# Two cross-attention layers on one core: two products split a second time, bias sums moved to ScalarE and DMA, first loads reordered

## The chip, the core and the metric

The kernel runs on one core of a Trainium2 chip. The metric is the time on the device in microseconds (us): 641.56 as the median of three runs (641.52 to 641.75). All data are float32.

TensorE (PE; its weight loads are shown as PEld) multiplies into PSUM, VectorE (DVE) and ScalarE (ACT) work on SBUF and PSUM, GpSimd (POOL) on SBUF. SyncE (SP), ScalarE and GpSimd issue DMAs. Each engine takes its instructions from a queue of its own.

## The reference

Eight batches of 100 queries with 1024 features attend to 1444 context rows with 512 features, twice. The second layer has no output product, and it normalises its result.

```
# layer 0
Q = x @ Wq + bq;  K = ctx @ Wk + bk;  V = ctx @ Wv + bv
w = softmax(Q @ K.T / 32, axis=-1)          # over the context
x = x + (w @ V) @ Wo + bo
# layer 1
q = x @ Wq + bq;  k = ctx @ Wk + bk;  v = ctx @ Wv + bv
w = softmax(q @ k.T / 32, axis=1)           # over the queries
y = w @ v + x
out = (y - mean(y)) * rsqrt(var(y) + 1e-6) * gamma + beta
```

## The kernel before

The scores need only Wq Wk^T (1024 x 512) and not Wq and Wk each, so the kernel multiplies weights first: **qk0** = Wq Wk^T of layer 0, **vo0** = Wv Wo (512 x 1024), and later **qk1** = Wq Wk^T of layer 1. The biases enter as vectors: Wq bk, Wk bq and Wo^T bv. The stages are qk0, vo0, the projected queries g0 of layer 0 (`queries`), qk1, the rounds of layer 0 (in each, `alternated` interleaves the weighted sum A of one batch, L531, with the scores s of the batch two further on, L560), the output product of layer 0, the projected queries of layer 1, the rounds of layer 1, and the normalisation.

**Seven products instead of eight.** Each weight product (`weight_products`, L241) is cut in quarters A11 .. A22 and B11 .. B22 and computed by Strassen's method in Winograd's form. The products are called X, Z, Y, W, and X again twice and Y again, as two banks of PSUM are used once more; the results that are finished in between are copied out by ScalarE (`put`, L296) or added by VectorE (`add`, L301). The sums and differences of quarters (`combine`, L165) are VectorE's. For qk0 and qk1 a product is sixteen matmuls of 256 columns, for vo0 eight of 512. The order on TensorE is the program's:

```
X = A11 B11;  Z = A12 B21;  Y = S1 T1;  W = A22 T4;  X += S2 T2;  X += S3 B12';  Y += S4 B22
```

with S1 = A21 + A22, T1 = B12 - B11, T2 = B22 - T1, T4 = B21 - T2, S2 = S1 - A11, S3 = A11 - A21, S4 = A12 - S2. Most sums overwrite a quarter that is not needed any more. An "X +=" goes into banks that `put` has just copied, so its first matmul waits for that copy. The last "X +=" (line L348) is called V below.

**Loads.** The contraction of 1024 is cut in eight units (tag `unit`, ten buffers), each with its rows of the left and the right matrix; a unit of a later product is loaded when a buffer is free. All these loads are issued by SyncE, except the first two by ScalarE (L254). For qk0 they come in the order of L255 to L263: left half and the whole right row of each unit, then the second left halves.

**Bias vectors.** `accumulate` (L305) multiplies each unit by a column of the bias and adds up the eight units on VectorE, one instruction for each (L318, L320), in rows of 1024 (tag `row`, three buffers) or 512. `block_sums` (L355) transposes blocks of 32 and reduces them, and `totals` (L363) sums over the partitions with a matmul on TensorE.

TensorE's order is the program's (`manual_schedule`). On the other engines a scheduler places instructions by priority and expected readiness, except those passed through `keep_in_program_order`. A buffer of a tag is free when its last reader is done. The tiles `prob` (three) hold scores; their rows from 96 on and their columns from 1444 on are cleared by GpSimd at the start (L135, L136). `weight_rows` (tag `wT`, three buffers) are used from the first softmax on.

Of the kernel before, what the change touches and what calls it, by code (L numbers as in the profile page):

```python
# [25 lines left out]
F32 = mybir.dt.float32  # L26
AF = mybir.ActivationFunctionType
# [28 lines left out]
def two_layer_cross_attention(ctx: ExitStack, tc: tile.TileContext, a: dict, out: bass.AP):  # L56
# [11 lines left out]
    def bank(name):  # L68
        return psum.tile([P, 512], F32, tag="ps", name=name)

    def bank2(name):
        return psum2.tile([P, 512], F32, tag="ps2", name=name)
# [59 lines left out]

    prob = [const.tile([P, SW], F32, tag=f"prob{n}", name=f"prob{n}") for n in range(3)]
    for t in prob:
        nc.gpsimd.memset(t[T // QD * QD :, :], 0.0)  # L135
        nc.gpsimd.memset(t[:, S:], 0.0)  # L136

    def run(*parts):

        parts = list(parts)  # L140
        while parts:
            parts = [g for g in parts if next(g, parts) is not parts]
# [7 lines left out]

    def half_product(banks, lhs, rhs, fresh, nb, width):

        per = nb // len(banks)
        for i in range(len(lhs)):
            for n in range(nb):
                nc.tensor.matmul(  # L156
                    banks[n // per][:, n % per * width : (n % per + 1) * width],
                    lhs[i][:, n * P : (n + 1) * P],
                    rhs[i],
                    start=(fresh and i == 0 and n % per == 0),  # L160
                    stop=(i == len(lhs) - 1),
                    skip_group_check=True,
                )

    def combine(to, x, y, op, engine=vector):  # L165
        for t, p, q in zip(to, x, y):
            engine.tensor_tensor(t, p, q, op)
# [19 lines left out]
    def seven_products(name, A, Bs, S, T_, nb, width, put, add, left=None, right=None):  # L187
# [49 lines left out]
        add(0, 1, Y)  # L237
        yield


    def weight_products(name, left, right, l_width, r_width, scaled):  # L241

        H, lh, rh = EC // 2, l_width // 2, r_width // 2
        nb, per = lh // P, 512 // rh
        lsrc = a[left].rearrange("(p c) n -> p c n", c=EC)
        rsrc = a[right].rearrange("(p c) n -> p c n", c=EC)  # L250
        units = [unit(f"{name}_{h}") for h in range(EC)]
        if name == "qk0":
            for part in (slice(0, lh // 2), slice(lh // 2, lh)):
                nc.scalar.dma_start(out=units[0][:, part], in_=lsrc[:, 0, part])  # L254
            nc.sync.dma_start(out=units[0][:, l_width : l_width + rh], in_=rsrc[:, 0, :rh])  # L255
            for h in range(1, EC):
                nc.sync.dma_start(out=units[h][:, :lh], in_=lsrc[:, h, :lh])
                nc.sync.dma_start(out=units[h][:, l_width : l_width + r_width], in_=rsrc[:, h, :])
                if h == 1:
                    nc.sync.dma_start(out=units[0][:, l_width + rh : l_width + r_width], in_=rsrc[:, 0, rh:])  # L260
            for i in range(H):
                for h in (i, H + i):
                    nc.sync.dma_start(out=units[h][:, lh:l_width], in_=lsrc[:, h, lh:])  # L263
        else:
            for h in range(EC):
                nc.sync.dma_start(out=units[h][:, :l_width], in_=lsrc[:, h, :])
                nc.sync.dma_start(out=units[h][:, l_width : l_width + r_width], in_=rsrc[:, h, :])

        def lefts(k, j):
            return [units[k * H + i][:, j * lh : (j + 1) * lh] for i in range(H)]  # L270

        def rights(k, j):
            return [units[k * H + i][:, l_width + j * rh : l_width + (j + 1) * rh] for i in range(H)]

        A11, A12, A21, A22 = lefts(0, 0), lefts(1, 0), lefts(0, 1), lefts(1, 1)
        B11, B12, B21, B22 = rights(0, 0), rights(0, 1), rights(1, 0), rights(1, 1)
        extra = [wide(f"{name}_s{n}").rearrange("p c t -> p (c t)") for n in range(2)]
        S1 = [extra[i // 2][:, i % 2 * 768 : i % 2 * 768 + lh] for i in range(H)]
        T1 = [extra[i // 2][:, i % 2 * 768 + lh : (i % 2 + 1) * 768] for i in range(H)]

        dst = weights.tile([P, l_width // P, r_width], F32, tag="w", name=name)

        def pair(n):
            return [(bank2 if n == "w" else bank)(f"{name}_{n}{j}") for j in range(2)]

        def product(banks, lhs, rhs, fresh):
            half_product(banks, lhs, rhs, fresh, nb, rh)

        def block(r, c, j):

            n = r * nb + j * per
            return dst[:, n : n + per, c * rh : (c + 1) * rh]

        def put(r, c, banks):
            for j in range(2):
                nc.scalar.copy(block(r, c, j), banks[j].rearrange("p (n w) -> p n w", n=per))  # L296

        def add(r, c, banks):
            for j in range(2):
                to = block(r, c, j)  # L300
                nc.vector.tensor_tensor(to, to, banks[j].rearrange("p (n w) -> p n w", n=per), ALU.add)  # L301

        accs = {}

        def accumulate(side):  # L305
            for v, of in scaled:
                if of != side:
                    continue
                width = (l_width, r_width)[side]
                if width == E:  # L310
                    acc = row(f"{name}_{v}")
                else:
                    acc = work.tile([P, L], F32, tag="half", name=f"{name}_{v}", bufs=1)
                accs[v] = acc
                for h in range(EC):
                    src = units[h][:, :l_width] if side == 0 else units[h][:, l_width : l_width + r_width]
                    if h == 0:
                        nc.vector.tensor_scalar(acc, src, cols[v][:, h : h + 1], None, ALU.mult)  # L318
                    else:
                        nc.vector.scalar_tensor_tensor(acc, src, cols[v][:, h : h + 1], acc, ALU.mult, ALU.add)  # L320

        X = pair("x")
        product(X, A11, B11, True)
        put(0, 0, X)
        combine(T1, B12, B11, ALU.subtract)
        combine(S1, A21, A22, ALU.add)
        Z = pair("z")
        product(Z, A12, B21, True)
        accumulate(1)
        add(0, 0, Z)  # L330
        Y = pair("y")
        product(Y, S1, T1, True)
        put(1, 1, Y)
        combine(B11, B22, T1, ALU.subtract)
        T2 = B11
        combine(B21, B21, T2, ALU.subtract)
        W = pair("w")
        product(W, A22, B21, True)
        put(1, 0, W)
        combine(S1, S1, A11, ALU.subtract)  # L340
        S2 = S1
        combine(B12, B22, B12, ALU.subtract)
        product(X, S2, T2, False)
        put(0, 1, X)
        accumulate(0)
        combine(A21, A11, A21, ALU.subtract)
        combine(A12, A12, S2, ALU.subtract)
        product(X, A21, B12, False)  # L348
        add(1, 0, X)
        add(1, 1, X)  # L350
        product(Y, A12, B22, False)
        add(0, 1, Y)
        return dst, [accs[v] for v, _ in scaled]

    def block_sums(name, t, sums):  # L355

        nc.vector.transpose(t, t)  # L360
        nc.vector.tensor_reduce(sums, t.rearrange("p (c q i) -> p c q i", q=P // QD, i=QD), AX.X, ALU.add)

    def totals(name, sums, n):  # L363
# [10 lines left out]
    def quarter_sums(name):  # L374
        return small.tile([P, 2 * EC, P // QD], F32, tag="sums", name=f"{name}_sums")
# [87 lines left out]
    for g in range(B // G):  # L463
# [9 lines left out]
    block_sums("wqbk0", acc_c, sums_c[:, :EC, :])  # L473
    gT = [None, None]
    gT[0], steps = queries(0, wqk0, totals("u0", sums_u, LC))
    run(steps)
    block_sums("bvo", acc_o, sums_c[:, EC:, :])
    got = totals("wqbk0", sums_c, 2 * EC)
    wqbk0 = got[:, :EC]
    nc.vector.tensor_tensor(out_bias, out_bias, got[:, EC:], ALU.add)  # L480
    kb0 = [key_bias_sums(f"kb0_{g}", g * GT, (g + 1) * GT, wqbk0) for g in range(B // G)]
    wqk1, (acc_c, acc_u) = weight_products(
        "qk1", "L1_xattn_WqT", "L1_xattn_WkT", E, L, (("L1_xattn_bk", 0), ("L1_xattn_bq", 1))
    )
    c0 = key_biases("c0", kb0, bqbk0)
    for e in range(EC):
        nc.gpsimd.tensor_scalar(xT[:, e, :], xT[:, e, :], out_bias[:, e : e + 1], None, ALU.add)  # L487
    sums = quarter_sums("k1")
    block_sums("u1", acc_u, sums[:, :LC, :])
    block_sums("wqbk1", acc_c, sums[:, LC : LC + EC, :])  # L490
    got = totals("k1", sums[:, : LC + EC, :], LC + EC)
    u1, wqbk1 = got[:, :LC], got[:, LC:]


    def load_features(b):

# [345 lines left out]
    for b in range(B):  # L842
        if b == B - 1:

            o0 = list(project0(AS, A0))
            next(o0[0])
            next(o0[0])
        run(alternated(b, 0, softmax0, A0[b // G][:, :, b % G * T : (b % G + 1) * T]))
        if b == 1:
            AS = value_sums(wvo)  # L850
    next(o0[1])
    for steps in o0:
# [67 lines left out]
```

## Time and profile before

| what | us |
|---|---|
| median of three runs | 641.56 |
| the profiled execution | 642.15 |
| its span, first to last instruction | 640.30 |
| TensorE busy | 628.8 |
| VectorE busy | 457.0 |
| ScalarE busy | 132.1 |
| GpSimd busy | 101.8 |

The mean granted clock of TensorE was 0.996. Busy time by stage, from the windows of the trace (columns: stretch, its length, PE, DVE, ACT, POOL busy, DMA in GB/s):

| stretch | stage | length | PE | DVE | ACT | POOL | GB/s |
|---|---|---|---|---|---|---|---|
| 0 to 20.9 | qk0, X and Z | 20.9 | 17.86 | 13.58 | 2.46 | 8.82 | 313 |
| 20.9 to 55.8 | qk0, the rest | 34.9 | 34.90 | 33.66 | 3.52 | 0.00 | 240 |
| 55.8 to 104.2 | vo0 | 48.4 | 48.40 | 40.74 | 4.69 | 0.00 | 126 |
| 104.2 to 142.0 | g0 | 37.8 | 37.80 | 25.37 | 4.76 | 0.00 | 72 |
| 142.0 to 190.7 | qk1 | 48.7 | 48.70 | 34.09 | 4.69 | 20.82 | 77 |
| 190.7 to 210.4 | first scores | 19.7 | 19.70 | 8.53 | 6.95 | 0.00 | 354 |
| 210.4 to 232.0 | round 0 | 21.6 | 21.60 | 16.22 | 6.82 | 0.00 | 277 |
| 232.0 to 254.0 | round 1 | 22.0 | 22.00 | 12.13 | 7.79 | 0.00 | 314 |

How to read it: the times of a row are of one execution under the profiler. A matmul of float32 shows as two records. The ends of matmuls are modelled, and the records of neighbours overlap, so the length of a stage is better read from the chain of work than from a sum of records. "Idle before" in a row is the time its engine stood before it, with what released it.

### The profile page before, as it was taken

To read this page: it belongs to the slowest core of one execution; us is meant where nothing else is said; L and a number is where in the kernel's file an instruction comes from. 1 tells how busy PE (TensorE), PEld (TensorE's weight loads), DVE (VectorE), ACT (ScalarE), POOL (GpSimd) and SP (SyncE) were. 2 spreads that over 40 slices of the span, in tenths; PEclk is the share of its full clock that TensorE was granted. 3 is DMA by queue.
4 is the path that set the end of the run, shared out by engine and by line. 5 is a ranking of instruction groups with operands and counts; after the bars stand their busy time and mean duration, and the time that the engine had idled before them with its cause. 6 is when DMAs were issued, how large, how long until landed. Compare 5 with 4: busy or idle time off the path is not lost.

```text
span 640.3 us, 9944 instructions
## 1 busy us (share of the span) xinstructions
PE 628.8 (98%) x3968; PEld 518.0 (81%) x3968; DVE 457.0 (71%) x864; ACT 132.1 (21%) x337; POOL 101.8 (16%) x118
## 2 busy tenths in 40 slices
PE   8999999999999999999999999999999999999994
PEld 7886445568885999999998655556999999999992
DVE  5999959569823775666655798229786659898886
ACT  1010010100103333212330000123332340325301
POOL 5000000009200000000010000007212220454054
PEclk9999999999999999999999999999999999999998
DMA  9928019000079799899896303046788990599002
GB/s 290 384 86 333 0 49 340 0 1 0 2 268 364 264 320 302 306 314 323 300 336 214 126 1 131 2 156 212 265 308 306 310 321 35 193 329 333 28 20 83
DMA packets 47907, 127.28 MB, mean 199 GB/s; under 512 B 3890, under 2 KB 6450, under 8 KB 47862
## 3 DMA queue, kind: packets, MB, share of 16 engines
q1 hardware_dynamic: 45784, 120.85, 54.6%
q0 software_dynamic: 1680, 5.33, 2.4%
q8 instruction: 31, 0.51, 0.3%
q10 hardware_dynamic: 398, 0.47, 0.2%
q14 instruction: 14, 0.11, 0.1%
HBM read 123.36 MB, written 3.28 MB: 198 GB/s over the span
## 4 chain that ended last, share of the span: by engine, by line
PE 94%; DVE 2%; issue 1%; DMA 1%; POOL 1%; POOLq 0%; SPq 0%; ACT 0%; DVEq 0%
PE s L560 25%; PE A L531 24%; PE qk_x L156 5%; PE g_x L156 5%; PE o_x L156 5%; PE qk_y L156 4%; PE g_y L156 3%; PE vo_x L156 3%; PE o_y L156 3%; PE qk_w L156 2%; PE vo_y L156 2%; PE g_w L156 2%; PE g_z L156 2%; PE o_w L156 2%; PE o_z L156 2%; PE qk_z L156 1%
## 5 line engine op out<-in xcount | busy, mean ns | idle before, releaser
L531 PE MATMUL A<-w,c 120*128 120x100 f32 (+1 forms) x1536 | 247.5, 265 | 0.0
L531 PEld LDWEIGHTS A<-w,c 120*128 120x128 f32 (+1 forms) x1536 | 215.9, 190 | 0.8
L93 DVE STREAM_TRANSPOSE w<-prob 32x384 f32<-32x384 f32 (+1 forms) x256 | 143.7, 561 | 37.3 <-ACT prob L572 15.1
L560 PE MATMUL s<-cT,g1T 128*100 128x131 f32 (+2 forms) x592 | 122.8, 297 | 0.0
L560 PE MATMUL s<-cT,g0T 128*100 128x131 f32 (+2 forms) x592 | 122.7, 296 | 0.0
L560 PEld LDWEIGHTS s<-cT,g1T 128*100 128x100 f32 x592 | 78.3, 167 | 8.9 <-ACT g1T L436 0.9
L560 PEld LDWEIGHTS s<-cT,g0T 128*100 128x100 f32 x592 | 78.3, 167 | 8.3
L572 ACT ACTIVATE prob<-s,c 100x393 f32<-100x393 f32 (+2 forms) x64 | 35.1, 560 | 116.7 <-PE s L560 116.4
L682 ACT ACTIVATE w<-w,negmax 120x100 f32<-120x100 f32 (+1 forms) x96 | 34.8, 364 | 82.3 <-DVE negmax L93 82.3
L487 POOL TENSOR_SCALAR xT<-xT,L_xattn_bo 128x800 f32<-128x800 f32 x8 | 20.8, 2609 | 134.0 <-PE qk_x L156 134.0
L592 DVE TENSOR_REDUCE maxima<-prob 100x1 f32<-100x394 f32 (+3 forms) x32 | 16.6, 528 | 28.1 <-ACT prob L572 27.9
L156 PE MATMUL qk_x<-qk 128*128 128x256 f32 x128 | 29.0, 382 | 1.0 <-DMA qk<-in_L_xattn_WkT 1.0
L701 POOL TENSOR_TENSOR part<-w 120x500 f32<-120x500 f32 x8 | 10.9, 1365 | 112.9 <-DVE rstd L776 28.6
L156 PEld LDWEIGHTS qk_x<-qk 128*128 128x128 f32 x128 | 23.7, 190 | 5.3 <-DMA qk<-in_L_xattn_WqT 1.3
L865 POOL DMA_DIRECT2D vectors<-in_L_xattn_gamma x1 | 0.6, 604 | 163.2 <-DMA c<-in_ctx 163.2
L320 DVE SCALAR_TENSOR_TENSOR qk_L_xattn_bk<-qk,L_xattn_bk,qk_L_xattn_bk 128x1024 f32<-128x1024 f32 x14 | 17.9, 1277 | 3.3 <-DMA qk<-in_L_xattn_WqT 3.2
L436 ACT ACTIVATE g1T<-g_x,k 128x400 f32<-128x400 f32 x6 | 3.6, 594 | 74.2 <-PE g_x L156 63.8
L93 DVE TENSOR_TENSOR xT<-xT,o_x 128x400 f32<-128x400 f32 (+1 forms) x32 | 15.9, 540 | 3.9 <-PE o_x L156 3.7
L682 ACT ACTIVATION_READ_ACCUMULATOR w<-w,negmax 120x1 f32 (+1 forms) x96 | 17.9, 187 | 0.0
L781 POOL TENSOR_TENSOR z<-z,vectors 100x1024 f32<-100x1024 f32 x7 | 16.5, 2352 | 8.2 <-ACT z L780 8.2
L759 PE MATMUL z<-ident,xT 128*100 128x128 f32 x64 | 16.3, 273 | 0.0
L93 DVE TENSOR_TENSOR w<-w,rtotal 120x400 f32<-120x400 f32 (+1 forms) x24 | 15.6, 649 | 0.7
(212 smaller groups left out, 869.4 us busy)
## 6 DMA issues: line engine op xcount, KB each, us to landing
cT<-in_ctxT SPq DMA_DIRECT2D x64, 722.0 KB, 6.6
c<-in_ctx SPq DMA_DIRECT2D x48, 768.0 KB, 8.5
c<-in_ctx SPq DMA_DIRECT2D x16, 512.0 KB, 6.8
vo<-in_L_xattn_Wo SPq DMA_DIRECT2D x8, 512.0 KB, 5.4
qk<-in_L_xattn_WqT SPq DMA_DIRECT2D x8, 512.0 KB
qk<-in_L_xattn_WqT SPq DMA_DIRECT2D x15, 256.0 KB, 5.4
qk<-in_L_xattn_WkT SPq DMA_DIRECT2D x15, 256.0 KB, 6.3
c<-in_ctx SPq DMA_DIRECT2D x16, 224.0 KB, 6.5
```

The source lines that it names most:

```text
L93: ins = getattr(nc.vector, op)(*args, **kw)
L156: nc.tensor.matmul(banks[n // per][:, n % per * width : (n % per + 1) * width], lhs[i][:, n * P : (n + 1) * P], rhs[i], start=(fresh and i ...
L320: nc.vector.scalar_tensor_tensor(acc, src, cols[v][:, h : h + 1], acc, ALU.mult, ALU.add)
L487: nc.gpsimd.tensor_scalar(xT[:, e, :], xT[:, e, :], out_bias[:, e : e + 1], None, ALU.add)
L531: nc.tensor.matmul(ps[:, k * T : (k + 1) * T], c[m // CQ][:r, m % CQ, k * P : (k + 1) * P], w[:r, m, :], start=(m == 0 and k == 0), stop=( ...
L560: nc.tensor.matmul(banks[n // per][:T, cuts[n] - o : cuts[n + 1] - o], q[:, k, t0 : t0 + T], cT[k][:, cuts[n] : cuts[n + 1]], start=(k == ...
L572: nc.scalar.activation(p[:, part], ps[:T, : part.stop - part.start], AF.Identity, bias=key_bias[layer][:T, b : b + 1], scale=SCALE,)
L592: nc.vector.tensor_reduce(maxima[:, n : n + 1], p[:, part], AX.X, ALU.max)
L682: nc.scalar.activation(w[:r, m0 + m, :], w[:r, m0 + m, :], AF.Exp, bias=negmax[:r, m : m + 1], accum_out=total[:r, m : m + 1])
L701: add(part, w[:MR, 0:5, :], w[:MR, 5:10, :], ALU.add)
L759: nc.tensor.transpose(ps[:T, e * P : (e + 1) * P], xT[:, 4 * j + e, b * T : (b + 1) * T], ident)
L781: nc.gpsimd.tensor_tensor(z, z, beta[:T], ALU.add)
```

## The change

It does four things.

1. **qk0.** The loads come in the products' order: left halves and right first halves of all units, then the right second halves, then the second left halves (those of A22 ahead of those of A21). On TensorE, W follows Z, ahead of Y; T2 and T4 get tiles of their own (`weight_rows`). The bq sum is placed behind Z's addition and the bk sum behind the "X +=" with S2.
2. **vo0 and qk1.** W leaves its place behind Y. It is computed by `inner_product`: seven products of half the size in each direction, again in Winograd's form, interleaved with V (two matmuls of V for qk1, one for vo0, then one inner product, seven times). T2 and T4 are still written over B11 and B21.
3. **Bias rows of 1024 in vo0 and qk1** are no longer summed by VectorE. `transferred_sum` has ScalarE write eight scaled tiles, three of them into `prob`, and seven DMAs of GpSimd add them up in three levels. For vo0 this stands behind Z, for qk1 behind Y's copies.
4. **Moved steps.** The rows of `prob` are cleared behind qk1. The bv block sums are placed behind the fifth product of g0 and their total's matmul ahead of its last one, and the block sums of layer 1 (u1 and wqbk1) and their total come in the first rounds of layer 0.

The diff, cut to its core (the line numbers are those of the file before and after):

```diff
@@ -237,6 +241,57 @@
+    def inner_product(name, lhs, rhs, nb, width, put, add):
+        h, w = nb // 2, width // 2
+        A11, A12, A21, A22 = ([lhs[2 * k + i][:, c] for i in range(2)] for c in halves(nb * P) for k in range(2))
+        B11, B21, B12, B22 = ([rhs[2 * k + i][:, c] for i in range(2)] for c in halves(width) for k in range(2))
+        t = work.tile([P, LC, GT], F32, tag="gT", name=f"{name}_t", bufs=3).rearrange("p c t -> p (c t)")
+        S1 = [t[:, i * h * P : (i + 1) * h * P] for i in range(2)]
+        T1 = [t[:, 2 * h * P + i * w : 2 * h * P + (i + 1) * w] for i in range(2)]
+        combine(S1, A21, A22, ALU.add)
+        combine(T1, B12, B11, ALU.subtract)
+        combine(A21, A11, A21, ALU.subtract)
+        combine(B12, B22, B12, ALU.subtract)
+        def product(ps, left, right, fresh):
+            half_product([ps], left, right, fresh, h, w)
+        X = bank(f"{name}_x")
+        product(X, A11, B11, True)
+        put(0, 0, X)
+        yield
+        Z = bank2(f"{name}_z")
+        product(Z, A12, B21, True)
+        add(0, 0, Z)
+        combine(B11, B22, T1, ALU.subtract)
+        combine(A11, S1, A11, ALU.subtract)
+        yield
+        Y = bank(f"{name}_y")
+        product(Y, S1, T1, True)
+        put(1, 1, Y)
+        combine(B21, B21, B11, ALU.subtract)
+        combine(A12, A12, A11, ALU.subtract)
+        yield
+        product(X, A11, B11, False)
+        put(0, 1, X)
+        yield
+        W = bank2(f"{name}_w")
+        product(W, A22, B21, True)
+        put(1, 0, W)
+        yield
+        product(Y, A12, B22, False)
+        add(0, 1, Y)
+        yield
+        product(X, A21, B12, False)
+        add(1, 1, X)
+        add(1, 0, X)
+        yield
+    def halves(n):
+        return slice(0, n // 2), slice(n // 2, n)
     def weight_products(name, left, right, l_width, r_width, scaled):
...
@@ -252,15 +307,16 @@
         if name == "qk0":
             for part in (slice(0, lh // 2), slice(lh // 2, lh)):
                 nc.scalar.dma_start(out=units[0][:, part], in_=lsrc[:, 0, part])
             nc.sync.dma_start(out=units[0][:, l_width : l_width + rh], in_=rsrc[:, 0, :rh])
             for h in range(1, EC):
                 nc.sync.dma_start(out=units[h][:, :lh], in_=lsrc[:, h, :lh])
-                nc.sync.dma_start(out=units[h][:, l_width : l_width + r_width], in_=rsrc[:, h, :])
-                if h == 1:
-                    nc.sync.dma_start(out=units[0][:, l_width + rh : l_width + r_width], in_=rsrc[:, 0, rh:])
+                nc.sync.dma_start(out=units[h][:, l_width : l_width + rh], in_=rsrc[:, h, :rh])
             for i in range(H):
                 for h in (i, H + i):
-                    nc.sync.dma_start(out=units[h][:, lh:l_width], in_=lsrc[:, h, lh:])
+                    nc.sync.dma_start(out=units[h][:, l_width + rh : l_width + r_width], in_=rsrc[:, h, rh:])
+            for h in [H + i for i in range(H)] + list(range(H)):
+                nc.sync.dma_start(out=units[h][:, lh:l_width], in_=lsrc[:, h, lh:])
         else:
             for h in range(EC):
...
@@ -307,57 +376,101 @@
                 if of != side:
                     continue
                 width = (l_width, r_width)[side]
+                first = 0 if side == 0 else l_width
+                srcs = [(units[h][:, first : first + width], cols[v][:, h : h + 1]) for h in range(EC)]
+                if width == E and name != "qk0":
+                    accs[v] = transferred_sum(f"{name}_{v}", srcs)
+                    continue
                 if width == E:
                     acc = row(f"{name}_{v}")
                 else:
                     acc = work.tile([P, L], F32, tag="half", name=f"{name}_{v}", bufs=1)
                 accs[v] = acc
-                for h in range(EC):
-                    src = units[h][:, :l_width] if side == 0 else units[h][:, l_width : l_width + r_width]
+                for h, (src, by) in enumerate(srcs):
                     if h == 0:
-                        nc.vector.tensor_scalar(acc, src, cols[v][:, h : h + 1], None, ALU.mult)
+                        tc.keep_in_program_order(nc.vector.tensor_scalar(acc, src, by, None, ALU.mult))
                     else:
-                        nc.vector.scalar_tensor_tensor(acc, src, cols[v][:, h : h + 1], acc, ALU.mult, ALU.add)
+                        nc.vector.scalar_tensor_tensor(acc, src, by, acc, ALU.mult, ALU.add)
         X = pair("x")
         product(X, A11, B11, True)
         put(0, 0, X)
         combine(T1, B12, B11, ALU.subtract)
-        combine(S1, A21, A22, ALU.add)
-        Z = pair("z")
-        product(Z, A12, B21, True)
-        accumulate(1)
-        add(0, 0, Z)
+        if name == "qk0":
+            t2, t4 = (weight_rows(f"{name}_t{n}") for n in (2, 4))
+            T2, T4 = ([t[:, i * rh : (i + 1) * rh] for i in range(H)] for t in (t2, t4))
+            Z = pair("z")
+            product(Z, A12, B21, True)
+            combine(T2, B22, T1, ALU.subtract)
+            combine(T4, B21, T2, ALU.subtract)
+            combine(S1, A21, A22, ALU.add)
+            add(0, 0, Z)
+            accumulate(1)
+            W = pair("w")
+            product(W, A22, T4, True)
+            put(1, 0, W)
+        else:
+            combine(S1, A21, A22, ALU.add)
+            Z = pair("z")
+            product(Z, A12, B21, True)
+            accumulate(1)
+            add(0, 0, Z)
         Y = pair("y")
         product(Y, S1, T1, True)
         put(1, 1, Y)
-        combine(B11, B22, T1, ALU.subtract)
-        T2 = B11
-        combine(B21, B21, T2, ALU.subtract)
-        W = pair("w")
-        product(W, A22, B21, True)
-        put(1, 0, W)
+        if name != "qk0":
+            accumulate(0)
+            T2, T4 = B11, B21
+            combine(T2, B22, T1, ALU.subtract)
+            combine(T4, B21, T2, ALU.subtract)
         combine(S1, S1, A11, ALU.subtract)
         S2 = S1
         combine(B12, B22, B12, ALU.subtract)
         product(X, S2, T2, False)
         put(0, 1, X)
-        accumulate(0)
+        if name == "qk0":
+            accumulate(0)
+            W = iter(())
+        else:
+            W = inner_product(f"{name}_w", A22, T4, nb, rh, put_part, add_part)
         combine(A21, A11, A21, ALU.subtract)
         combine(A12, A12, S2, ALU.subtract)
-        product(X, A21, B12, False)
+        V = half_steps(X, A21, B12, False, nb, rh)
+        for _ in range(7):
+            run(islice(V, 2 * nb // 4))
+            next(W, None)
+        run(V)
         add(1, 0, X)
         add(1, 1, X)
         product(Y, A12, B22, False)
         add(0, 1, Y)
         return dst, [accs[v] for v, _ in scaled]
-    def block_sums(name, t, sums):
-        nc.vector.transpose(t, t)
+    def transferred_sum(name, srcs):
+        tiles = [row(f"{name}_{n}") for n in range(2)] + [weight_rows(f"{name}_{n}")[:, :E] for n in range(2, 5)]
+        tiles += [t[:, :E] for t in prob]
+        for t, (src, by) in zip(tiles, srcs):
+            tc.keep_in_program_order(nc.scalar.activation(t, src, AF.Copy, scale=by))
+        n = 1
+        while n < EC:
+            for i in range(0, EC, 2 * n):
+                nc.gpsimd.dma_start(out=tiles[i], in_=tiles[i + n], accum_op=ALU.add)
+            n *= 2
+        return tiles[0]
+    def block_sums(name, t, sums, late=False):
+        ins = nc.vector.transpose(t, t)
+        if late:
+            tc.keep_in_program_order(ins)
         nc.vector.tensor_reduce(sums, t.rearrange("p (c q i) -> p c q i", q=P // QD, i=QD), AX.X, ALU.add)
...
@@ -473,24 +586,22 @@
     block_sums("wqbk0", acc_c, sums_c[:, :EC, :])
     gT = [None, None]
     gT[0], steps = queries(0, wqk0, totals("u0", sums_u, LC))
+    run(islice(steps, 5))
+    block_sums("bvo", acc_o, sums_c[:, EC:, :], late=True)
+    run(islice(steps, 1))
+    got = totals("wqbk0", sums_c, 2 * EC)
     run(steps)
-    block_sums("bvo", acc_o, sums_c[:, EC:, :])
-    got = totals("wqbk0", sums_c, 2 * EC)
     wqbk0 = got[:, :EC]
     nc.vector.tensor_tensor(out_bias, out_bias, got[:, EC:], ALU.add)
     kb0 = [key_bias_sums(f"kb0_{g}", g * GT, (g + 1) * GT, wqbk0) for g in range(B // G)]
     wqk1, (acc_c, acc_u) = weight_products(
         "qk1", "L1_xattn_WqT", "L1_xattn_WkT", E, L, (("L1_xattn_bk", 0), ("L1_xattn_bq", 1))
     )
+    for t in prob:
+        nc.gpsimd.memset(t[T // QD * QD :, :], 0.0)
     c0 = key_biases("c0", kb0, bqbk0)
     for e in range(EC):
         nc.gpsimd.tensor_scalar(xT[:, e, :], xT[:, e, :], out_bias[:, e : e + 1], None, ALU.add)
-    sums = quarter_sums("k1")
-    block_sums("u1", acc_u, sums[:, :LC, :])
-    block_sums("wqbk1", acc_c, sums[:, LC : LC + EC, :])
-    got = totals("k1", sums[:, : LC + EC, :], LC + EC)
-    u1, wqbk1 = got[:, :LC], got[:, LC:]
     def load_features(b):
@@ -846,7 +957,13 @@
             next(o0[0])
             next(o0[0])
         run(alternated(b, 0, softmax0, A0[b // G][:, :, b % G * T : (b % G + 1) * T]))
+        if b == 0:
+            sums = quarter_sums("k1")
+            block_sums("u1", acc_u, sums[:, :LC, :], late=True)
+            block_sums("wqbk1", acc_c, sums[:, LC : LC + EC, :], late=True)
         if b == 1:
+            got = totals("k1", sums[:, : LC + EC, :], LC + EC)
+            u1, wqbk1 = got[:, :LC], got[:, LC:]
             AS = value_sums(wvo)
     next(o0[1])
     for steps in o0:
```

## The prediction

> **What bounds the kernel now.** First the head of the page, then its chain by engine.
>
> ```profile
> span 640.3 us, 9944 instructions
> PE 628.8 (98%) x3968; PEld 518.0 (81%) x3968; DVE 457.0 (71%) x864; ACT 132.1 (21%) x337; POOL 101.8 (16%) x118
> PE 94%; DVE 2%; issue 1%; DMA 1%; POOL 1%; POOLq 0%; SPq 0%; ACT 0%; DVEq 0%
> ```
>
> TensorE is the bound, so only two things shorten the run: less time on TensorE, or a smaller gap in it. The chain in order of time shows where gaps are (columns: start, length, what):
>
> ```profile
> 2.16 5.58 DMA qk<-in_L_xattn_WkT
> ...
> 20.13 0.70 DVE qk_s L93
> 20.82 0.04 issue
> 20.87 7.17 PE qk_y L156 x32
> 28.04 6.91 PE qk_w L156 x32
> ...
> 76.57 6.87 PE vo_w L156 x16
> ```
>
> Before 20.87 the chain is DMA and VectorE; from there to about 621 it is TensorE alone. So all gaps that can be won lie before 20.87. TensorE's own timeline of that stretch:
>
> ```profile
> 4.43 3.86 PE L156 MATMUL qk_x<-qk 128*128 128x256 f32 x16
> 9.26 3.69 PE L156 MATMUL qk_x<-qk 128*128 128x256 f32 x16 [0.97 <-DMA qk<-in_L_xattn_WkT]
> 12.78 7.08 PE L156 MATMUL qk_z<-qk 128*128 128x256 f32 x32
> ```
>
> An undisturbed product of this size takes 6.91 (the qk_w row), so the first two, X and Z, could end at 4.43 + 13.82 = 18.25. They end at 19.86: 1.6 us go to late loads (the second row starts at 9.26, after a wait for Wk^T), and 1.0 more until Y, which waits for VectorE's sums.
>
> Then the later part of the chain, for the widths and for the place that the change reorders:
>
> ```profile
> 156.00 6.91 PE qk_y L156 x32
> 162.91 6.91 PE qk_w L156 x32
> 169.81 13.89 PE qk_x L156 x64
> ...
> 327.71 11.59 PE A L531 x104
> ```
>
> Two records make one matmul. A product of sixteen 256-wide matmuls costs 6.91 / 16 = 0.432 each; 52 matmuls of width 100 cost 11.59 / 52 = 0.223 each.
>
> Last, ScalarE around the second Wq Wk^T, with TensorE's weight loads, and the one row in which ScalarE scales a 1024-wide tile:
>
> ```profile
> 162.08 0.59 ACT L296 COPY qk<-qk_y 128x512 f32<-128x512 f32 x1 [12.36 <-PE qk_y L156]
> 162.94 0.59 ACT L296 COPY qk<-qk_y 128x512 f32<-128x512 f32 x1 [0.28 <-PE qk_y L156]
> ...
> 175.89 0.59 ACT L296 COPY qk<-qk_x 128x512 f32<-128x512 f32 x1 [5.46 <-PE qk_x L156]
> 176.53 6.77 PEld L156 LDWEIGHTS qk_x<-qk 128*128 128x128 f32 x32 [0.21 <-ACT qk L296]
> ```
>
> ```profile
> L780 ACT ACTIVATE z<-z,rstd x7: 1148/1149/1152, 555.1 to 629.6; 100x1024 f32<-100x1024 f32 x7
> ```
>
> To be seen: the last X product accumulates into the banks that ScalarE has just copied out, and its weight load waits for the copy. Today ScalarE is idle 5.46 before it, so the wait is 0.21.
>
> [...] The page's plain 512 KB loads from GpSimd took 5.5 and 6.1; an accumulating one is in no row.
>
> **The change, part by part** (times of the profiled execution: span 640.30, run 642.15).
>
> *First loads and order of qk0.* X and Z now wait for left halves and right first halves: 384 KB a unit instead of 512, 3.15 MB instead of 4.19 (MB of a million bytes). The rate in two-us stretches was 298, 280, 288, 336, 332, 389, 384, 388 GB/s from 2 on, so 1.18 MB (three units, new order) is in by 6.0, and 1.57 MB (old order) by 7.35. The old third unit was usable at 9.2, a lag of 1.9; the new one comes at 7.9, when TensorE, after two units of 1.73 from 4.43, is at 7.89. The fourth: 1.57 MB, 9.2, needed at 9.6. Later units come with growing reserve. So X and Z end near 18.4. W takes Y's place behind them; it needs T4, made of the right second halves (4.19 MB), and its first A22 (4.46 MB: 15.5, + 1.9 lag, + 0.7 because eight issues of 128 KB at 0.43 each feed only 300 GB/s: 18.1). Twelve VectorE sums of 0.34 run as halves land. W starts at 18.4 where Y started at 20.87: **-2.4**. Bounds: -2.5 (18.25 with nothing late), -1.0 (loads as before, only Y's wait gone). Y then starts 6.9 later, A21 lands by 22 + 1.9, and the VectorE queue, bq sums included, has some 2 us in hand up to Y's end: nothing.
>
> *Split of Wv Wo's W.* Eight 512-wide matmuls (6.87) become seven products of two 256-wide ones: 14 x 0.432 = 6.05: **-0.8**. Its small sums on VectorE have 0.9 to 3 us each before they are read, covered by the V matmuls in between.
>
> *Split of the second W.* Sixteen 256-wide (6.91) become 28 of 128 x 128. No row has this form. [...] the last projections' 150-wide rows are 0.255. I take 0.223: 6.24, **-0.7** (bounds -0.9, +0.2).
>
> *ScalarE bias sums.* Taking eight 1.2 us sums per product from VectorE is worth nothing by itself: VectorE ended no wait after 20.87. What they cost is their place. For Wv Wo they queue between the copies of X (end 62.88 + 0.59) and of Y (75.75): 8 x 1.15 = 9.2 fit in 12. For the second Wq Wk^T they are queued behind Y's copies and ahead of the copies of the next X product. W no longer lies between these, so that product directly follows Y. In the old clock: Y's copies end at 163.53; eight activations [...] without overlap at 172.8; a copy of 0.59 and a handoff follow (175.89 to 176.56: 0.67), so the next X product starts at 172.7 to 173.4. The X product behind Y ends its matmuls at 162.74 + 6.91 = 169.65. TensorE stands with nothing to do, since the interleaved W comes behind the first V step: **+3.1** (3.0 to 3.7). VectorE is late by less: I find its S2 ready 0.7 ahead, and any lateness there hides under this stand.
>
> *Accumulating DMAs, moved loads.* Seven of 512 KB per sum, three levels deep, on GpSimd's queue. Behind them are the clearing of prob, first written 8 us into the scores (199.03 - 190.8), and a freed row on which a VectorE sum waits in the middle of the split W. The first is sent near 165.8 old clock, behind two activations; VectorE reaches that wait near 176 and TensorE feels it after 179, 13.5 later. I take 5.5 to 11 (the plain row, and double): nothing, covered. The second weights' loads come earlier, since units go free earlier; the bias adds on GpSimd start some 6 us earlier. The u1 sums and part of the value sums, about 12 us of VectorE, move into the first score rounds, where it was busy 16.2 of 21.6 and 12.1 of 22; softmax has a full round in hand: nothing. The total's matmul (0.24) only moves.
>
> **Sum:** -2.4 - 0.8 - 0.7 + 3.1 = -0.8: span 639.5, run 641.35. The median shown, 641.56, is 0.6 under the profiled run, so I predict **640.8**.
>
> **Rivals.** (a) *ScalarE does not hold TensorE*: its eight activations fit or start earlier. For: ScalarE is idle 5.46 before each of these copies. Against: 6.1 us of room for 8.5. Then -3.9: 637.7. (b) *Slower, by the accumulating DMAs*: one that takes over 13.5 us stops VectorE inside the split W. Beyond that each us is a us; at 14.3 the gain is gone, at 18 it is -0.8 + 4.5: 645.3. Against: 5.5 for the plain row. (c) *The loads do not come sooner*[...]: only Y's wait is won, -1.0 instead of -2.4: 642.2.
>
> **How the numbers follow.** Forecast 0.62, (a) 0.20, (b) 0.10, (c) 0.08. A difference under 0.2% (1.3 us) is about what a measurement can't tell from none. The forecast's own range is 639.9 to 642.3; a fifth of it and a bit lies beyond -1.3, 0.14, so faster is 0.34. Slower: (b) and a corner of the forecast and (c), 0.13. Same: 0.53. The range 637.6 to 642.6 takes in most of (a) and (c) and leaves out (b).
>
> **What would show it.** In the changed profile: W first matmul at 18.4 or so, no TensorE gap between 20 and the second Wq Wk^T; vo's V and W together 12.9, the second's 13.1; one gap of about 3 us after the next-to-last X product there, released by ScalarE, with eight 1.1 us activations ahead of the copy. It would be wrong if that gap is missing, if narrow matmuls cost 0.25 or more, or if TensorE waits anywhere for VectorE behind an accumulating DMA.

## The result, and the profile after

| kernel | median us | runs | ratio to the kernel before, 95% interval |
|---|---|---|---|
| before | 641.45 | 20 | |
| changed | 642.89 (640.78 to 644.59) | 20 | 1.0019 (1.0010 to 1.0028) |

The changed kernel is slower by 1.4 us, 0.19%. The forecast was 640.8, the range up to 642.6, so both missed. In the profiled execution (642.59) the head of the page and the chain by engine read:

```profile
span 640.4 us, 10120 instructions
PE 628.4 (98%) x4004; PEld 522.4 (82%) x4004; DVE 451.0 (70%) x888; ACT 148.9 (23%) x357; POOL 114.3 (18%) x132
PE 95%; ACT 1%; issue 1%; POOL 1%; DVE 1%; POOLq 0%; DVEq 0%; ACTq 0%
```

ScalarE, at 0% of the chain before, now has 1%. The chain in order of time shows where (start, length, what):

```profile
18.68 6.91 PE qk_w L159 x32
...
161.20 4.25 ACT qk_L_xattn_bk L457 x4
165.46 3.12 ACT prob L457 x3
```

The gaps at the start are gone: W starts at 18.68 (18.52 in TensorE's timeline) where Y started at 20.87. In their place stands a piece of ScalarE, inside qk1. ScalarE's timeline there:

```profile
159.67 0.59 ACT L352 COPY qk<-qk_y 128x512 f32<-128x512 f32 x1 [0.28 <-PE qk_y L159]
160.15 5.31 ACT L457 ACTIVATE qk_L_xattn_bk<-qk,L_xattn_bk 128x1024 f32<-128x1024 f32 x5
165.36 3.21 ACT L457 ACTIVATE prob<-qk,L_xattn_bk 128x1024 f32<-128x1024 f32 x3
168.48 1.04 ACT L352 COPY qk<-qk_x 128x512 f32<-128x512 f32 x2
```

And TensorE's, from the X product with S2 on:

```profile
159.47 7.07 PE L159 MATMUL qk_x<-qk,qk_s 128*128 128x256 f32 x32
169.09 2.08 PE L159 MATMUL qk_x<-qk 128*128 128x256 f32 x4 [2.56 <-ACT qk L352]
170.96 1.57 PE L159 MATMUL qk_w_x<-qk 128*128 128x128 f32 x8
172.37 1.03 PE L159 MATMUL qk_x<-qk 128*128 128x256 f32 x4
173.23 1.05 PE L159 MATMUL qk_w_z<-qk 128*128 128x128 f32 x8
174.12 1.03 PE L159 MATMUL qk_x<-qk 128*128 128x256 f32 x4
```

Eight activations lie between Y's copies and X's, without a gap, and TensorE stands 2.56 us until the first X copy is made. That is the wait the prediction named. What it did not have is the line after: the first four V records take 1.87 us from start to start (169.09 to 170.96), where the same four take 0.86 further on (172.37 to 173.23), and the first small product takes 1.41 (170.96 to 172.37) instead of 0.89 (173.23 to 174.12). Together this is 1.5 us more. The windows of the trace say why (columns: stretch, its length, PE busy, granted TensorE clock, DMA share, GB/s):

```profile
168.00:168.50 0.50, 0.00 (x0) 1.00 1.10 205
168.50:169.00 0.50, 0.00 (x0) 0.61 1.04 188
169.00:169.50 0.50, 0.41 (x1) 0.50 0.79 139
...
171.00:172.00 1.00, 1.00 (x6) 0.50 1.04 193
172.00:172.50 0.50, 0.50 (x6) 0.97 0.78 139
```

While TensorE stands, its clock falls to half (0.50). A mean of 0.61 over the half microsecond from 168.50 puts the drop at 168.61, 2.1 us after the last matmul, and 0.97 in the stretch from 172.00 puts the return at 172.02 or 172.03. The clock stays low for 3.41 us, of which TensorE has work in 2.9; half of that is the 1.5 us lost.

By stage, from first record to first record on TensorE in each profile (the start up to the first vo0 record; qk1 up to the total's matmul ahead of the scores):

| kernel | start | vo0 | g0 | qk1 | rest |
|---|---|---|---|---|---|
| before | 55.73 | 48.23 | 38.01 | 48.48 | 449.8 |
| changed | 53.28 | 47.41 | 38.06 | 51.93 | 449.7 |

The start gains 2.45 and vo0 0.82; qk1 loses 3.45 and takes both back. These two executions differ by only 0.1 us of span, where the medians of all differ by 1.4: this profile of the kernel before is of a long execution, as the last experiment shows.

### The profile page after: what moved, and what is told of

Read it like the earlier page. It is cut to its first block, busy times and chain, and to the rows that moved or that the text cites. A ratio compares the mean times of both kernels' runs of the same rounds, so it can differ in the third digit from the quotient of the medians.

```text
span 640.4 us, 10120 instructions
## 1 busy us (share of the span) xinstructions
PE 628.4 (98%) x4004; PEld 522.4 (82%) x4004; DVE 451.0 (70%) x888; ACT 148.9 (23%) x357; POOL 114.3 (18%) x132
## 4 chain that ended last, share of the span: by engine, by line
PE 95%; ACT 1%; issue 1%; POOL 1%; DVE 1%; POOLq 0%; DVEq 0%; ACTq 0%
PE s L671 25%; PE A L642 24%; PE qk_x L159 6%; PE g_x L159 5%; PE o_x L159 5%; PE qk_y L159 4%; PE g_y L159 3%; PE vo_x L159 3%; PE o_y L159 3%; PE qk_z L159 2%; PE vo_y L159 2%; PE g_w L159 2%; PE g_z L159 2%; PE o_w L159 2%; PE o_z L159 2%; PE qk_w L159 1%
## 5 line engine op out<-in xcount | busy, mean ns | idle before, releaser
L159 PE MATMUL qk_x<-qk 128*128 128x256 f32 x128 | 30.6, 390 | 2.6 <-ACT qk L352 2.6
L891 ACT ACTIVATE z<-z,rstd 100x1024 f32<-100x1024 f32 x7 | 8.0, 1150 | 31.9 <-POOL rstd L888 31.9
```

Of the source, the lines that this page charges most:

```text
L159: nc.tensor.matmul(banks[n // per][:, n % per * width : (n % per + 1) * width], lhs[i][:, n * P : (n + 1) * P], rhs[i], start=(fresh and i ...
L891: nc.scalar.activation(z, z, AF.Copy, scale=rstd)
```

## Experiments

The theory: ScalarE's queue makes TensorE stand in qk1, and a spell at half clock follows. Rivals: the stand counts with its own length only; or the loss lies in the accumulating DMAs, the added instructions or the moved reductions.

**The activations ahead of Y's copies.** ScalarE is idle for 12.4 us before Y's copies, which is where the eight fit.

```diff
         product(Y, S1, T1, True)
+        if name != "qk0":
+            accumulate(0)
         put(1, 1, Y)
         if name != "qk0":
-            accumulate(0)
             T2, T4 = B11, B21
```

> The eight scaling activations of the second Wq Wk^T stand ahead of the Y copies in ScalarE's queue, where it is idle for about 12 us, instead of behind them; nothing is left out. Theory (a stand of TensorE of 2.6 us behind ScalarE's queue, and then a spell at half clock that costs another 1.7): both go, about -4.4 against the changed kernel's 642.9, so 638.5 (638.0 to 639.3), 3 us below the kernel before. Rival one (the stand costs its own length and no more, the rest of the loss lies outside the span or in the score rounds): 640.2. Rival two (the accumulating DMAs or their instructions are the loss, wherever ScalarE starts them): 642 to 643.

Measured: 639.71, ratio to the kernel before 0.9973 (0.9963 to 0.9983), 3.2 below the changed kernel. This is outside the theory's 638.0 to 639.3 and, as a number, nearer to the 640.2 of rival one. The profile decides: no V record is slow, and no gap is left to ScalarE. Most of the 1.2 us missing against 638.5 is visible in TensorE's timeline, where the X product with S2 is broken:

```profile
160.12 5.42 PE L159 MATMUL qk_x<-qk,qk_s 128*128 128x256 f32 x24
165.71 1.99 PE L159 MATMUL qk_x<-qk,qk_s 128*128 128x256 f32 x8 [0.17 <-DVE qk_s L93]
167.54 1.11 PE L159 MATMUL qk_x<-qk 128*128 128x256 f32 x4
```

From 160.12 to the first V record at 167.54 it takes 7.42 instead of 6.91, and it starts 0.27 late, 0.8 in all. In VectorE's timeline the four sums for V (A11 - A21), which need not wait for ScalarE's late reads any more, now run from 153.70 on, ahead of those for S2; the last S2 sum is over at 165.66, where the changed kernel has 160.36.

**The same with VectorE's order kept.** Beside the edit above, the sums of qk1 from S2 on are passed through `keep_in_program_order`.

```diff
+        vector.in_order = name == "qk1"
         combine(S1, S1, A11, ALU.subtract)
...
         combine(A12, A12, S2, ALU.subtract)
+        vector.in_order = False
```

> As the kernel with the activations ahead of Y's copies, but VectorE's sums of the second Wq Wk^T from S2 on keep the program's order, so that the four sums for V (A11 - A21), which the earlier activations set free, no longer go ahead of S2's. Nothing is left out. If VectorE's order is what that kernel lacked: the X product with S2 follows Y at once and takes 6.91, its stage takes about 47.9 instead of 48.57, and the time is 0.7 to 0.8 lower, 638.8 to 639.1, as with the gap filled. If something else holds it: 639.7 again.

Measured: 646.65, ratio 1.0076 (1.0062 to 1.0090). Both expectations missed. VectorE's timeline has the reason:

```profile
165.21 0.76 DVE L93 TENSOR_TENSOR o_s<-vo 128x256 f32<-128x256 f32 x2 [5.18 <-DMA qk_L_xattn_bk<-qk_L_xattn_bk]
```

The scheduler has put a value sum of layer 0's output between the sums for S2. It is written to a row that the accumulating DMAs still read, and VectorE, with S2's other sums behind it, stands 5.18 us. This is rival (b)'s mechanism. In the changed kernel the same value sum starts at 168.38 and does not wait. TensorE follows:

```profile
166.63 8.17 PE L159 MATMUL qk_x<-qk,qk_s 128*128 128x256 f32 x24 [4.89 <-DVE qk_s L93]
```

It stands 4.89 us for VectorE, and the 24 records behind it take 8.01 instead of 5.18, as the clock is at half from 165.35 to 172.18, 6.83 us. So the spell needs no wait for ScalarE: a stand behind VectorE brings it too. That VectorE's order is what the version before this one lacked stays a reading of its trace; this trial replaced that wait by a greater one.

**Other work in the gap.** ScalarE's queue is left as it is; TensorE gets three small products to do.

```diff
-        for _ in range(7):
+        for n in range(7):
+            if name == "qk1" and n == 0:
+                run(islice(W, 3))
             run(islice(V, 2 * nb // 4))
             next(W, None)
```

> ScalarE's queue stays as in the changed kernel, with the late copies; three of the seven small products of the split W in the second Wq Wk^T (3 x 0.89 = 2.7 us of TensorE work) run before the first V matmul instead of between the V matmuls, so that TensorE has work while it waits for the copies; nothing is left out. Theory: TensorE doesn't stand, so no half clock either: -4.4, 638.5 (638.3 to 639.5, as the second and third small product may wait some tenths for VectorE). Rival one (only the stand's own length counts): 640.2. Rival two (the loss isn't TensorE's wait for ScalarE): 642 to 643.

Measured: 638.77, ratio 0.9960 (0.9948 to 0.9971), 4.1 below the changed kernel. The late copies are still there (ScalarE copies X at 169.66 in this profile), but TensorE's timeline has no gap:

```profile
160.65 7.07 PE L159 MATMUL qk_x<-qk,qk_s 128*128 128x256 f32 x32
167.55 1.05 PE L159 MATMUL qk_w_x<-qk 128*128 128x128 f32 x8
...
170.28 1.13 PE L159 MATMUL qk_x<-qk 128*128 128x256 f32 x4
```

Work of 2.7 us in the gap gave back 4.1 us, and the stage shows the same: 47.84 instead of 51.93. This refutes the rival by which the stand counts only its length (640.2), and it is the fastest version found: 2.6 us below the kernel before.

**A shorter stand.** The loop that writes the scaled tiles is called ahead of Y's copies, stops after the first one and goes on behind these copies (the diff shows the loop alone).

```diff
...
-        for t, (src, by) in zip(tiles, srcs):
+        early = 8 if name[:3] == "vo0" else 1
+        for h, (t, (src, by)) in enumerate(zip(tiles, srcs)):
+            if h == early:
+                yield
             tc.keep_in_program_order(nc.scalar.activation(t, src, AF.Copy, scale=by))
...
```

> One of the eight activations of the second Wq Wk^T is put ahead of the Y copies, seven stay behind them; nothing is left out. The stand of TensorE should shrink by one activation's pitch, 1.05 us, from 2.6 to 1.6. If the spell at half clock follows any stand, or the stand costs only its own length (rival one): -1.05, 641.8. If the spell needs a stand longer than about 2 us: -1.05 - 1.7, 640.1, with no V matmul at double time in the trace.

Measured: 640.68, ratio 0.9988 (0.9982 to 0.9994). One activation less in the way is worth 2.2 us, twice its 1.05; of the two numbers expected, 641.8 and 640.1, the second is nearer. TensorE's timeline:

```profile
169.16 1.13 PE L159 MATMUL qk_x<-qk 128*128 128x256 f32 x4 [1.52 <-ACT qk L352]
170.12 1.05 PE L159 MATMUL qk_w_x<-qk 128*128 128x128 f32 x8
```

The stand is 1.52, and the V records behind it run at the usual pace. No other of the 22 executions was profiled, but all have a mean clock of 0.996 or 0.997; the kernel before, which has no spell in qk1, has 0.995 to 0.998, and a spell of 3.41 us at half lowers the mean by 0.003.

**A longer stand.** Two repeats of the eighth activation behind the eight, and ahead of X's copies; so that these stay behind, the copies of qk1, X's first excepted, are passed through `keep_in_program_order` (not shown).

```diff
...
+        for _ in range(2 if name[:3] == "qk1" else 0):
+            tc.keep_in_program_order(nc.scalar.activation(tiles[7], srcs[7][0], AF.Copy, scale=srcs[7][1]))
...
```

> Two more activations (repeats of the eighth, same result) stand behind the eight and ahead of the copies of the second X product of the second Wq Wk^T; nothing is left out. The stand should grow by two pitches, 2 x 1.05 to about 4.7 us. Theory: the stand grows by 2.1 and a spell at half clock follows it: 645.0 if the spell is as long as before, up to 646.5 if it grows. Rival one: 645.0 with V matmuls at the usual 0.43 us each. Rival two (the stand isn't where the time goes): within 1 us of the changed kernel, 642 to 644.

Measured: 645.93, ratio 1.0069 (1.0057 to 1.0081), 3.0 above the changed kernel for 2.1 us of ScalarE. TensorE's timeline:

```profile
171.75 2.08 PE L159 MATMUL qk_x<-qk 128*128 128x256 f32 x4 [4.92 <-ACT qk L352]
173.62 1.92 PE L159 MATMUL qk_w_x<-qk 128*128 128x128 f32 x8
```

The windows of this profile:

```profile
169.00:169.50 0.50, 0.00 (x0) 0.69 1.11 197
...
176.00:176.50 0.50, 0.50 (x3) 0.99 0.85 164
```

By the same arithmetic the clock is low from 169.19 to 176.01: 6.82 us, twice 3.41. The rival with V at its usual pace is out: the first four V records take 1.87, as in the changed kernel.

**W whole again in qk1.** All else as in the changed kernel.

```diff
+        if name == "qk1":
+            W = pair("w")
+            product(W, A22, T4, True)
+            put(1, 0, W)
         combine(S1, S1, A11, ALU.subtract)
...
             accumulate(0)
+            W = iter(())
+        elif name == "qk1":
             W = iter(())
         else:
             W = inner_product(f"{name}_w", A22, T4, nb, rh, put_part, add_part)
```

> The changed kernel with the second Wq Wk^T's W product whole again and in its old place between Y and the second X product; all else, ScalarE's eight activations behind the Y copies included, stays. Theory: the 6.9 us of W lie again between Y's copies and the second X's, the activations fit, TensorE doesn't stand and no spell at half clock follows; the split's 0.67 is lost: 642.9 - 2.6 - 1.5 + 0.7 = 639.5. Rival one (the stand counts with its length only): 641.0. Rival two (the activations and accumulating DMAs are the loss): 642.9 + 0.7 = 643.6.

Measured: 639.18, ratio 0.9965 (0.9953 to 0.9978). The eight activations stand behind Y's copies as in the changed kernel and cost next to nothing, since W's 6.9 us lie between. Neither the activations nor the accumulating DMAs are the loss; taking W out from behind Y is, while the activations stand there.

**The start alone, and Wv Wo alone.** The first is the kernel before with the hunk of the loads and the branch for qk0; the second is the changed kernel with these and qk1 as before.

> The kernel before with only the first part of the change: the first weights' loads in the products' order and W ahead of Y in the first Wq Wk^T, with T2 and T4 in tiles of their own; no split product, no ScalarE sums. Prediction's step: -2.4, 638.9 from the 641.3 of the kernel before. What the traces of the changed kernel and of four of its variants suggest: X and Z follow each other at once, but the first X product takes 7.0 to 8.2 us instead of 6.9, since the clock isn't up yet and no wait for loads covers that, so -1.2 to -2.35, -1.8 on average: 639.5. Rival (the loads come no sooner): -1.0, 640.3.

> Of the change only the part at Wv Wo is left: its W product split in seven, its bias sum by ScalarE and accumulating DMAs, and the moved u1 and wqbk1 reductions and clearing of prob; first loads, both Wq Wk^T and their sums by VectorE as in the kernel before. Theory: the split gives 6.87 - 14 x 0.432 = 0.8, the sums and DMAs cost nothing: -0.8, 640.5. Rival (the accumulating DMAs, or the reductions moved into the score rounds, cost time of their own): 641.3 or more, as the split's gain is then eaten.

Measured: 639.85, ratio 0.9974 (0.9964 to 0.9983), for the start, and 640.50, ratio 0.9984 (0.9977 to 0.9990), for Wv Wo, against 641.55. The first number lies between the 639.5 of the theory and the 640.3 of the rival and does not decide; the profile has X, Z and W one behind the other without a gap and the first vo0 record at 53.40. So the start is worth 1.7 of the 2.4 forecast, and Wv Wo 1.05 where 0.8 was forecast; its stage is shorter by 0.82 in the profile, as in every kernel with the split.

**Both kernels once more.** They are profiled again to see what in the start differs between executions.

> The kernel before, unchanged, for a second profile of its start. If the prediction's start step was too large because its one profile of the kernel before was a slow one (span 640.3, against a median of 639.2 to 639.6 in its other executions): no wait of 0.97 us for Wk^T inside the first X product, Y at about 19.8 instead of 20.87, and a span near 639.4. If that profile was typical and the changed start simply gives less: the wait is there again and Y starts at 20.6 to 20.9.

> The changed kernel, unchanged, for a second profile: its executions range over 3.2 us of span, 638.6 to 641.8. Theory: the stand of 2.6 us is there in each, and the spread is the length of the half-clock spells (none to 1.5 us behind the stand, 0.1 to 1.4 us in the first X product). A span near 639 should then show no V matmul at double time, a span near 641.5 both spells long. Rival: the stand's own length varies.

> The changed kernel once more, for a third profile, with the same question and the same expectations as the second: the stand stays at 2.6 us, and what differs between executions is how long TensorE runs at half clock behind it and at the start.

Measured: 640.91 (span 639.0), 643.16 (640.9) and 643.53 (641.1). In the second profile of the kernel before, TensorE's timeline has no wait for Wk^T:

```profile
1.06 3.78 PE L105 MATMUL warm<-ones 128*128 128x128 f32 x16 [1.06 <-DVE mhalf L120]
4.63 7.45 PE L156 MATMUL qk_x<-qk 128*128 128x256 f32 x32
...
19.34 7.17 PE L156 MATMUL qk_y<-qk_s 128*128 128x256 f32 x32 [0.35 <-DVE qk_s L93]
```

Y starts at 19.34, not 20.87. The Wv Wo kernel, which has the old load order, has 19.84 and no such wait either. So of three profiles with the old order only the first, which the prediction was made from, has the wait of 0.97 for a load; how many other executions have it is not known. In the changed kernel the stand is 2.56 in all three profiles, so between these its length does not vary; the low clock lasts 3.41 us in each and costs 1.5, 1.7 and 1.8. No profile caught one of the changed kernel's six executions (of twenty) with a span below 639.6, 638.6 to 639.5. But with the shortest start profiled the stages add up to 638.8 without any spell (53.28 + 47.41 + 38.06 + 47.85 + 2.56 + 449.6), so in these six there is room for some 0.7 us of it at most, if their other stages are as long. The mean clock agrees: 0.997 or 0.998 in four of them and 0.995 in two, where it is 0.994 or 0.995 in the other fourteen.

All stages of the profiles in one table, "stand" and "slow" being the gap and the extra time at half clock:

| kernel | start | vo0 | qk1 | stand | slow | qk1 less both |
|---|---|---|---|---|---|---|
| before, second profile | 54.20 | 48.23 | 48.48 | 0 | 0 | 48.48 |
| fill the gap | 54.45 | 47.42 | 47.84 | 0 | 0 | 47.84 |
| one activation early | 54.38 | 47.41 | 49.48 | 1.52 | 0 | 47.96 |
| changed | 53.28 | 47.41 | 51.93 | 2.56 | 1.52 | 47.85 |
| changed, second | 53.69 | 47.42 | 52.13 | 2.56 | 1.72 | 47.85 |
| changed, third | 53.81 | 47.41 | 52.18 | 2.56 | 1.76 | 47.86 |
| two more activations | 53.56 | 47.41 | 54.95 | 4.92 | 2.15 | 47.88 |
| sums first, order kept | 53.35 | 47.41 | 55.96 | 4.89 | 2.83 | 48.24 |

The last column closes the account: with the split, qk1 is 47.84 to 47.96 plus the stand plus the slow spell; only the last row has some 0.3 more, by which its X product with S2 starts late (0.2) and V behind it (0.1).

## Why the prediction was wrong

**First loads, W ahead of Y: "W starts at 18.4 where Y started at 20.87: -2.4".** The order came as described: W behind Z, and no gap up to qk1. The size failed, -1.7 measured. The figure 20.87 was from an execution whose span, 640.3, is above the median span of 639.2 to 639.6 in the executions of that kernel taken later; the two other profiles with the old order have 19.34 and 19.84, with no wait for a load in X and Z and 0.35 and 0.33 of waiting at Y instead of 1.01. The start alone reaches vo0 0.80 and 1.29 ahead of these two (54.20 and 54.69) and 2.33 ahead of the first. So what was mis-sized here is the 1.6 us of late loads and Y's wait: they were taken as every execution's. The prediction took 0.6 off the whole sum for a long execution, but the excess lay in the very gap that the change closes, so it was counted as a gain as well. And the other end moves: the first X product, taken at 6.91, takes 6.98 to 8.16 us up to Z's first record, since its matmuls first run at the pace of the warm ones (0.446 us for 128 columns, twice the later 0.2225). The changed start ends between 53.28 and 54.45.

**Split of Wv Wo's W: -0.8.** Right: -0.82 in the stage.

**Split of the second W: 0.223 each, -0.7.** Right: -0.64 (48.48 to 47.84), and eight records, four matmuls, take 0.89.

**"TensorE stands with nothing to do ... +3.1 (3.0 to 3.7)".** This is the step that failed. The place, the releaser and the reason were right. The stand itself was shorter, 2.56: the eight activations took 8.33 from their start to that of the copy (160.15 to 168.48), not 8.6, which was the author's estimate (eight at the 1.149 shown for one would be 9.2), and the gap shown counts from the end of the last record (166.54), 0.16 later than the 6.91 by which the prediction counted. But the cost of the stand is more than its length, and the sum has no term for the clock: it was put at nothing without a reason. A spell at half clock adds 1.5 to 1.8, so the term is +4.1 to +4.3, outside its bounds. The spells last 3.41 and 6.83 us in the traces. Here a stand of 2.56 us was enough in three profiles out of three, the clock falling 2.1 to 2.6 us after the last matmul.

**Accumulating DMAs: nothing, covered.** Right: they took 5.2 to 7.8 us from issue to landing (medians of their groups; "5.5 to 11" was taken), and the kernel without W's split in qk1, which has all of them, runs at 639.18. **Moved reductions: nothing.** Right within the error: the rest of the span is 449.5 to 450.1 in all profiles. **VectorE's lateness: hidden.** Right, and without the stand too: with the gap filled, TensorE waits for VectorE nowhere.

The sum of the steps is -1.7 - 1.05 - 0.64 + 2.56 + 1.7 = +0.9 for +1.4 measured; of the rest, some 0.2 lies outside the span (the time is 2.2 us over the span in the changed kernel's executions, 2.0 in the old one's), and the remainder is within the intervals of the two measured parts, some 0.6 each. Of the rivals, (a) and (b) did not happen: ScalarE did hold TensorE, and no accumulating DMA stopped VectorE in the changed kernel, though one did when its order was altered. (c), at 1.0, is no further from 1.7 than the forecast, by luck: on the whole the loads came no slower, the start alone, with rows of half the length for the right matrix, moving 289, 340 and 347 GB/s between 2 and 8 us, against 298, 280 and 288, and 306, 279 and 316, in the two profiles of the kernel before.

## What to carry to other kernels

Price a stand of TensorE at its length plus the half-clock work behind it: in the profiles 1.5 to 2.8 us more for stands of 2.6 us and over and nothing at 1.5, so that 1.05 us less of waiting was worth 2.2. When a buffer comes back after another engine's copy, look at all that stands ahead of that copy in its engine's queue, and give the waiting engine independent work, or put the queue's long part where that engine is idle. And before crediting a change with a gap, look at a second execution: the gap may be that execution's own.

## What the runs showed of the hardware

The trace also keeps the moments at which the granted clock changed. In the table, "first rise" is when it rose to full at the start, "between" the time from there to the drop, and "behind" how long after the end of the last matmul the drop came.

| kernel | stand | first rise | drop | between | behind | low for |
|---|---|---|---|---|---|---|
| changed | 2.56 | 4.77 | 168.61 | 163.84 | 2.07 | 3.41 |
| changed, second | 2.56 | 5.62 | 169.46 | 163.84 | 2.51 | 3.41 |
| changed, third | 2.56 | 5.85 | 169.69 | 163.84 | 2.62 | 3.41 |
| two more activations | 4.92 | 5.34 | 169.19 | 163.85 | 2.36 | 6.83 |
| sums first, order kept | 4.89 | 4.92 | 165.35 | 160.43 | 3.61 | 6.83 |
| one activation early | 1.52 | 6.99 | none | | | |

In each of these spells the clock is at half (0.50). The first rise comes at 4.19 to 7.15 in the thirteen profiles. The clock fell at stands of 2.56, 4.89 and 4.92 us and not at 1.52; between 1.52 and 2.56 no run decides. The drop did not come at a fixed time behind the last matmul, 2.07 to 3.61, while its time behind the first rise was 163.84 or 163.85 in four profiles and 3.41 less in the fifth. So a stand of 2.56 us may bring no spell where it lies otherwise in time. That is an estimate from this table, and would explain the six short executions; none of them was profiled.

The start follows the same record. Until the first rise the eight warm matmuls take 0.446 us each from start to start (1.06 to 4.63), twice the 0.2225 of the same shape later, and the first X product loses half of what is left up to the rise: 0.49, 0.61 and 1.16 us where the rise comes 0.99, 1.22 and 2.35 us behind its start (changed second and third, one activation early). The windows read 1.00 there only because the record begins with that rise.

An activation of 1024 columns shows 1.134 to 1.151 us, but eight in a row follow at 1.04 to 1.05: an overlap of 0.10. What lies between the span and the whole time, 1.8 to 2.5 us by kernel, was not looked into.
